# Two expert layers at the end of a metaformer kernel: four pairs of images in the second weight pass, expert outputs copied to token rows by TensorE, and a redrawn order

## The chip, the cores and the metric

The kernel runs on one core of a Trainium2 chip. The metric is the device time of one execution in microseconds (us), the median of several runs.

## What is computed

The input is x with shape (32, 56, 56, 128), fp32: 32 images of 3136 tokens with 128 channels. Two layers follow each other, each with a mixing step and a feed-forward step, all with residuals.

```python
x = x + L0_conv(_ln_c(x))            # batch norm, binarised 3x3 convolution
t = t + L0_ffn(_ln_t(t))             # 8 experts, each token uses its top 2
x = x + L1_conv(_ln_c(x))            # triangle-like product over each image
t = t + L1_ffn(_ln_t(t))             # 64 experts, each expert chooses 8 tokens
```

The change touches the last step. For each image, a softmax over the tokens gives each of the 64 experts its 8 best tokens with weights topv. An expert gets one vector per image, the weighted sum of these 8 tokens, runs it through two layers, and the result is added back to the same 8 tokens:

```python
pooled = jnp.einsum('bked,bke->bed', gathered, topv)
h = jax.nn.gelu(jnp.einsum('ebd,edh->ebh', h, weight1), approximate=False)
out = jnp.einsum('ebh,eho->ebo', h, weight2)
weighted = jnp.einsum('beo,bke->bkeo', out, topv)
outputs = outputs.at[batch, flat_idx].add(weighted)
```

So an expert (128x512 and 512x128 weights, 256 KB each in fp32) sees 32 vectors only, one per image. Two images can choose no common token, but two experts of one image can choose the same token, so additions to one image have to be ordered or summed first.

## The kernel before, in words

Images are handled in 16 pairs; a pair has 7 units of 896 tokens. A first sweep takes statistics of all images for the batch norm (up to about 330 us). Then the pairs flow through a pipeline of stages, several pairs at once: `fetch`, `sign`, `conv`, `conv_back` (convolution), `moe_turn`, `moe_gates`, `moe_experts`, `moe_add` (the 8 experts: a gate row is broadcast from DRAM into a tile gb at line 821, multiplied with the transposed tokens xT on VectorE at line 827, and multiplied with all experts' weights on TensorE at line 832, tile acc), `tri_*` (the product over an image), `gate_stats`, `gate_turn`, `gate_logits` (outputs to DRAM, logits for the 64 experts), `top8` (MAX8 and FIND_INDEX8 on VectorE, lines 1189 and 1193, then 8 gathers of token rows on POOL, line 1222) and `pool_rows` (the pooled vector per expert; its transpose on TensorE is line 1251 for the late pairs).

The 64 experts run in 16 groups of four, in two passes over all weights. The first pass (`late_experts(False, g)`) serves pairs 0 to 12 and begins when pair 12 is pooled; the second (`late_experts(True, g)`) serves the last NL = 3 pairs. Each group is: load weights (lines 1412, 1414), first layer `ph` (1479), a copy on ScalarE, a transpose `trh` (1503), bias (1511) and gelu (1519), second layer `po` (1525), output bias on VectorE (1533), and a store of 128x128 outputs to DRAM (1541).

What follows differs. In the first pass the outputs of a group are loaded back from DRAM, each image's row 8 times, into two tiles eo (line 1551, 8 loads a group on the SP queue; tag xT, the buffers that hold the transposed tokens), multiplied by topv (1558, one VectorE instruction of 112 or 96 rows x 512), and added to token rows in DRAM by 8 indirect DMAs with add (1575, on POOL). The images of the first pass form two lots (0 to 13 and 14 to 25); the scatters of one lot have to follow each other, those of two lots need not. When a scatter belongs to another lot than the one before it, POOL first runs a tiny memset (line 1316).

In the second pass nothing is scattered with add. `last_sums` makes per pair a matrix m of topv where two experts chose the same token (lines 1647, 1655) and gathers that pair's token rows, 8 gathers of 128 rows (1666). `last_load` brings the outputs of 32 experts to SBUF (1689); `last_out_rows` multiplies m by them on TensorE (1708), adds the rows (1720) and writes them with indirect DMAs (1731). It does so in two halves of 32 experts; the second half sums over all 64. Writes of one pair follow each other.

The order is drawn up by the kernel itself. A planner (`Order.run`) plays the whole program with a cost per operation (the numbers given to `op`, and `land` for a DMA's landing), chooses the next operation per engine by a rank, and emits the instructions in the order that results. The ranks come from `TICK`, a table of due times per stage and unit; PERIOD = 14 ticks separate two pairs. On the chip each engine runs its instructions strictly in that order and waits at the first one that is not ready; so does the SP queue with its DMA issues. Tiles come from tags with fixed numbers of buffers (x 15, u 6, ps 8 PSUM banks, gb 5, xT 4).

Of the kernel before, what the change touches and what calls it, by code (L numbers as in the profile page):

```python
# [12 lines left out]
F32 = mybir.dt.float32  # L13
# [14 lines left out]
C = 128  # L28
N7 = 7
# [9 lines left out]
    "fetch": (1.58, 3.45, 5.52, -1.97, 9.89, 8.41, 11.94),  # L39
    "sign": (-0.24, 0.69, 0.62, 6.29, 6.36, 10.44, 7.52),  # L40
    "conv": (1.26, 2.47, 6.82, 8.46, 10.49, 11.27, 13.74),
    "conv_back": (3.04, 3.74, 6.89, 9.11, 10.54, 11.48, 14.87),
    "moe_turn": (4.55, 4.08, 9.93, 10.17, 12.05, 12.07, 15.21),
    "moe_gates": (7.93, 6.46, 10.3, 10.32, 15.22, 13.8, 15.72),
    "moe_experts": (10.11, 8.23, 10.44, 10.38, 15.35, 13.82, 17.26),
    "moe_add0": (14.4, 13.58, 10.89, 13, 17.91, 16.49, 17.47),
    "moe_add1": (12.35, 12.05, 11.31, 12.55, 16.09, 14.74, 18.98),
    "tri_turn": (16.03, 16.94, 19.18, 18.34, 19.2, 18.97, 19.62),
    "moe_stats": (4.06, 9.6, 11.95, 15.11),
    "moe_route": (6.11, 10.25, 12.5, 15.67),  # L50
    "tri_stats": (14.43, 14.07, 18.68, 19.34),
    "tri_b": (20.52, 21.37),
    "tri_a": (22.17, 21.41),
    "tri_z": (22.19,),
    "tri_out": (23.45, 23.11, 25.14, 25.06, 25.81, 28.13, 29.03),
    "gate_stats": (23.81, 25.31, 26.89, 30.24),
    "gate_turn": (25.22, 25.8, 26.84, 28.27, 29.66, 32.16, 31.08),
    "gate_logits": (26.8, 27.15, 28.55, 30.19, 30.4, 34.44, 34.71, 34.72),
    "clear": (32.94,),
    "top8": (36.55,),  # L60
    "pool_rows": (39.18,),
    "late_first": (27.19, 27.47, 30.26, 33.5, 37.45, 38.24, 40.16, 41.35, 43.38, 44.86, 45.85,
        48.06, 49.55, 51.3, 58.28, 60.22),
    "late_alone": (47.43, 50.82, 50.84, 53.47, 61.88, 67.39, 57.81, 65.6, 63.21, 71.67, 75.8,
        82.21, 97.17, 84.67, 68.82, 79.34),
    "last_sums": (70.63, 74.49, 77.96),
    "last_load": (68.66, 101.21),
    "last_rows": (91.82, 76.74, 99.71, 103.42, 119.45, 116.33),
# [4 lines left out]
NX, NY = 15, 6  # L73
# [212 lines left out]
def kernel(ctx: ExitStack, tc: tile.TileContext, a: dict, out: bass.AP):  # L286
# [12 lines left out]
    HB = B // 2  # L299
# [23 lines left out]
    make_identity(nc, ident)  # L323

# [42 lines left out]
    NL = 3  # L367
    LAST = range(NP - NL, NP)
    HB = 2 * ((NP - NL + 1) // 2)
    LOTS = ((0, HB), (HB, B - 2 * NL)) + tuple((2 * p, 2 * p + 2) for p in LAST)  # L370
# [3 lines left out]
    EH = E1 // 2  # L374
# [4 lines left out]
    o_d = [dram.tile([NE, B, C], F32, name=f"o_{g}") for g in range(E1 // NE)]  # L379
# [25 lines left out]
    with ExitStack() as c2:  # L405
# [21 lines left out]
        for t in lines:  # L427
# [3 lines left out]
            "x": NX, "u": NY, "ps": 8, "gb": 5, "xT": 4, "yl": 3,  # L431
            "st": 3, "q": 3, "lg": 1, "k1": 1, "k2": 1, "mk": 2, "d": 2,
            "gg": 2, "gT": 2, "rm": 4, "zq": 1, "lgT": 1,
            "m8": 2, "i8": 2, "sq": 2, "pg": 4, "near": 2, "pacc": 1, "ptc": NL + 1,
# [155 lines left out]
        def fetch(p, u):  # L590
            g = p * NU + u
            x_ = live[p]["x", u] = new("x", [128, N7, C], f"x_{NUT + g}")

            @op("SP", 360, w=parts(x_), land=1200)
            def _():
                nc.sync.dma_start(x_.ap, x_units[g])

        def sign(p, u):
# [3 lines left out]
            @op("SP", 360, r=[("y1_d", g)], w=[y], land=1200)  # L602
            def _():
                nc.sync.dma_start(y.ap, y1_d[g])
# [205 lines left out]
        def moe_experts(p, u, n):  # L810
# [8 lines left out]
            @op("SP", 360, r=[("gd", p, u)], w=[gb], land=1300)  # L819
# [136 lines left out]
        def tri_z(p):  # L956
# [71 lines left out]
            @op("SP", 360, r=[(zT, 0), (zT, 4)], w=[("z_d", p)], land=300)  # L1028
# [12 lines left out]
            for rg in range(4):  # L1041
                @op("SP", 720, r=[("z_d", p), zv], w=[(zv, rg)], land=300)
# [86 lines left out]
        def gate_turn(p, u):  # L1129
# [6 lines left out]
            @op(*issue, r=parts(x_), w=[("out", p, u)], land=1200)  # L1136
# [7 lines left out]
            @op(*issue, r=parts(y), w=[("y3", p, u)], land=1200)  # L1144
# [1009 lines left out]
```

## Time and profile before

| | |
|---|---|
| three timed runs | 3786.0, 3786.38, 3797.89 us (median 3786.38) |
| profiled execution | 3805.24 us, its span 3803.4 us |
| busy of the span | PE 3427.8 us (90%), DVE 3191.5 (84%), ACT 2350.5 (62%), POOL 443.8 (12%) |
| mean granted TensorE clock | 0.96 |
| largest group | acc at L832: 12544 instructions, 1473.6 us |
| scatters of the first pass, L1575 | 128, mean 1548 ns, idle before them 317.1 us |
| loads of eo at L1551 | 128, median 781 ns of the SP queue each |
| DMA | 842 MB, mean 221 GB/s |

PE is TensorE's matmul stream, PEld its weight loads, DVE VectorE, ACT ScalarE, POOL GpSimd, SP the queue that issues most DMAs. In a row of groups or of the timeline, `out<-in` are the program's names, an xN at the end the number of merged instructions, and the bracket the idle time of the engine before it with what ended it. A fp32 matmul is two instructions.

### The profile page before, as it was taken

What the parts mean: (1) busy time and instruction counts of PE and PEld (TensorE: products, weight loads), DVE (VectorE), ACT (ScalarE), POOL (GpSimd) and SP (SyncE); (2) the same over time, 40 slices, a digit from 0 to 9 for tenths busy, and PEclk for the clock granted to TensorE, in tenths of its full rate; (3) what the DMA queues carried; (4) which work ended last, traced back from release to release, by engine and by line L of the source; (5) the groups of instructions that cost most, each with busy time, mean ns of one, the idle gap of its engine ahead of it and who ended that gap; (6) DMA issues with size and microseconds to landing.
All of it is one profiled execution on the core that took longest, in us unless ns stands there. A gap on an engine that the chain in (4) does not pass through costs nothing.

```text
span 3803.4 us, 79485 instructions
## 1 busy us (share of the span) xinstructions
PE 3427.8 (90%) x28051; PEld 2791.8 (73%) x28051; DVE 3191.5 (84%) x10626; ACT 2350.5 (62%) x5438; POOL 443.8 (12%) x506
## 2 busy tenths in 40 slices
PE   7998999999999999999999999999999997876644
PEld 7886878787877777777777777777777775664422
DVE  7997979898989898989898989898989886765551
ACT  6997357575757666666666666666666664453420
POOL 0000000101010101010101010101010104234454
PEclk9999999999999999999999999999999998898667
DMA  7996747474747474747474747474747477687685
GB/s 292 358 356 226 256 155 268 151 272 148 276 150 268 146 268 153 269 154 269 154 269 156 265 155 268 157 267 158 265 160 262 163 251 210 201 248 227 184 238 163
DMA packets 358127, 842.03 MB, mean 221 GB/s; under 512 B 89169, under 2 KB 133154, under 8 KB 357730
## 3 DMA queue, kind: packets, MB, share of 16 engines
q1 hardware_dynamic: 298658, 719.02, 54.8%
q10 hardware_dynamic: 38080, 99.57, 6.6%
q0 software_dynamic: 20992, 18.37, 2.9%
q8 instruction: 223, 3.65, 0.4%
q14 instruction: 174, 1.43, 0.1%
HBM read 661.53 MB, written 175.23 MB: 220 GB/s over the span
## 4 chain that ended last, share of the span: by engine, by line
PE 44%; DVE 27%; DMA 14%; ACT 8%; issue 3%; SPq 2%; POOL 1%; another core or an unknown queue 0%; ACTq 0%; POOLq 0%; DVEq 0%
PE acc L832 21%; DMA gb<-gate 7%; DVE gb L827 5%; DVE stln L488 5%; PE gram L1799 4%; PE ps_cv L633 4%; PE tr L477 3%; PE ps_g L1067 2%; ACT yt L562 2%; DVE frame L611 2%; DVE x L575 2%; DMA w_True<-in_L_ffn_weight 2%; PE ps_z L976 2%; DVE x L1111 1%; DVE sg L1102 1%
## 5 line engine op out<-in xcount | busy, mean ns | idle before, releaser
L832 PE MATMUL acc<-expert_w,gb 128*128 128x128 f32 x12544 | 1473.6, 278 | 73.0 <-DVE gb L827 49.2
L832 PEld LDWEIGHTS acc<-expert_w,gb 128*128 128x128 f32 x12544 | 1437.7, 193 | 121.7 <-DVE gb L827 51.4
L827 DVE TENSOR_TENSOR gb<-gb,xT 128x1024 f32<-128x1024 f32 x784 | 949.3, 1220 | 95.3 <-DMA gb<-gate 91.3
L488 DVE BATCH_NORM_STATS2 stln<-x 128x6 f32<-128x128 f32 x2352 | 600.1, 287 | 1.9
L562 ACT ACTIVATE yt<-x,rmln 128x128 f32<-128x128 f32 x784 | 327.2, 495 | 203.6 <-DVE rmln L550 190.0
L562 ACT ACTIVATE yl<-x,rmln 128x128 f32<-128x128 f32 x756 | 324.2, 494 | 175.7 <-DVE rmln L547 125.3
L633 PE MATMUL ps_cv<-frame,w_sign 128*128 128x448 bf16 x2016 | 420.0, 357 | 8.3 <-DVE frame L611 8.3
L562 ACT ACTIVATE ym<-x,rmln 128x128 f32<-128x128 f32 x784 | 324.6, 486 | 66.9 <-DVE rmln L550 57.3
L633 PEld LDWEIGHTS <-w_sign 128*128 128x128 bf16 x2016 | 196.5, 98 | 174.4 <-DVE frame L611 8.5
L1222 POOL DMA_INDIRECT rows<-y,near x128 | 133.2, 1041 | 995.5 <-DVE k L738 795.7
L1575 POOL DMA_INDIRECT out<-eo_False,picked x128 | 198.1, 1548 | 317.1 <-DMA out<-eo_False,picked 137.0
L1118 POOL MEMSET a_bd<- 128x2048 f32 x15 | 27.1, 1807 | 1655.4 <-PE ps_zo L1089 1655.4
L562 ACT ACTIVATE y<-x,rm 128x128 f32<-128x128 f32 x448 | 210.5, 716 | 14.5 <-DVE rm L547 14.5
L1067 PE MATMUL ps_g<-wg,yT 128*128 128x128 f32 x1568 | 211.2, 283 | 0.0
L1067 PEld LDWEIGHTS ps_g<-wg,yT 128*128 128x128 f32 x1568 | 192.0, 195 | 20.5 <-issue 12.0
L583 ACT COPY xT<-trm 128x512 f32<-128x512 f32 x224 | 110.1, 529 | 151.6 <-PE trm L477 132.7
L641 ACT ACTIVATE cv<-ps_cv,cv_shift,cv_scale 128x448 f32<-128x448 f32 x224 | 159.2, 726 | 70.7 <-PE ps_cv L633 36.1
L844 DVE TENSOR_TENSOR x<-acc,x 128x512 f32<-128x512 f32 (+1 forms) x224 | 139.7, 623 | 73.7 <-PE acc L832 62.8
L1799 PE MATMUL gram<-y 128*128 128x128 f32 x1568 | 198.4, 279 | 0.0
L1799 PEld LDWEIGHTS gram<-y 128*128 128x128 f32 x1568 | 194.4, 200 | 0.5 <-issue 0.5
L488 DVE BATCH_NORM_STATS2 st<-x 128x6 f32<-128x128 f32 x784 | 179.6, 282 | 4.6 <-DMA x<-in_x 4.6
L583 ACT COPY ylT<-trl 128x512 f32<-128x512 f32 x224 | 113.7, 533 | 111.4 <-PE trl L477 102.0
(263 smaller groups left out, 5439.5 us busy)
## 6 DMA issues: line engine op xcount, KB each, us to landing
gb<-gate SPq DMA_DIRECT2D x784, 512.0 KB
x<-in_x SPq DMA_DIRECT2D x224, 448.0 KB
y<-yT SPq DMA_DIRECT2D x112, 448.0 KB
ys<-y SPq DMA_DIRECT2D x112, 448.0 KB
out<-x ACTq DMA_DIRECT2D x105, 448.0 KB
y<-yl ACTq DMA_DIRECT2D x105, 448.0 KB
w_False<-in_L_ffn_weight SPq DMA_DIRECT2D x128, 256.0 KB
w_True<-in_L_ffn_weight SPq DMA_DIRECT2D x102, 256.0 KB
```

What stands on the lines that cost most here:

```text
L488: nc.vector.bn_stats(st.ap[:, c0 + k, :], src.ap[:, k, :])
L562: nc.scalar.activation(dst.ap[:, k, :], src.ap[:, k, :], AF.Identity, bias=m, scale=r)
L583: nc.scalar.copy(t.ap[:, n0 : n0 + k, :].rearrange("c n p -> c (n p)"), ps.ap[:, : k * 128],)
L633: nc.tensor.matmul(acc, lhsT=w_sign[:, tap, :], rhs=frames[f][:, 8 * band + kh : 8 * band + kh + 8, kw : kw + W], start=(tap == 0), stop=( ...
L641: nc.scalar.activation(cv.ap[:, :, 64 * h : 64 * h + 64], ps.ap[:, :448].rearrange("c (q n) -> c n q", n=N7), AF.Identity, bias=cv_shift, ...
L827: nc.vector.tensor_tensor(gb.ap, gb.ap, over(xT.ap[:, n, :], E0), ALU.mult)
L832: nc.tensor.matmul(acc.ap[:, n % 4 * C : (n % 4 + 1) * C], lhsT=gb.ap[:, e, :], rhs=expert_w[:, e * C : (e + 1) * C], start=(e == 0), stop ...
L844: nc.vector.tensor_tensor(dst, acc.ap[:, : k * C], dst, ALU.add)
L1067: nc.tensor.matmul(psg.ap[:, n * C : (n + 1) * C], lhsT=yT[:, n0 + n, 16 * u : 16 * u + 16, :].rearrange("c r v -> c (r v)"), rhs=wg, star ...
L1222: nc.gpsimd.indirect_dma_start(out=rows.ap[:, j, :], out_offset=None, in_=y3_d[p], in_offset=bass.IndirectOffsetOnAxis(ap=near.ap[:, k + j ...
L1575: ins = nc.gpsimd.indirect_dma_start(out=tokens_out, out_offset=bass.IndirectOffsetOnAxis(ap=picked[lot][:rows, e : e + 1], axis=0), in_=e ...
L1799: nc.tensor.matmul(gram.ap[:, :C], lhsT=y.ap[:, n, :], rhs=y.ap[:, n, :], start=(g % G16 == 0 and n == 0), stop=(g % G16 == G16 - 1 and n ...
```

## The change

The number of pairs in the second pass goes from 3 to 4, so the first pass serves pairs 0 to 11 and its two lots are 12 images (96 rows) each. The first pass keeps its outputs on the chip: a constant `spread` of 128 x 2 x 96, built at the start from the identity by 8 VectorE copies, is multiplied on TensorE with the outputs of each expert (32 rows), which gives each image's row 8 times in PSUM; VectorE multiplies by topv on the way to eo, now per expert and lot, in 4 buffers of a tag of its own; xT has 3 buffers. The store to DRAM and the loads back go away in the first pass. In the second pass the final rows are made for 48 experts first and then for 16, and the fourth pair's rows live in eo buffers. Landing times given to the planner change at many DMAs, and all of TICK is redrawn, for the early stages as well.

```diff
-    "late_first": (27.19, 27.47, 30.26, 33.5, 37.45, 38.24, 40.16, 41.35, 43.38, 44.86, 45.85,
-        48.06, 49.55, 51.3, 58.28, 60.22),
+    "late_first": (27.83, 31.72, 32.41, 37.47, 41.1, 43.48, 47.62, 49.5, 49.91, 52.26, 56.62,
+        60.45, 61.11, 64.22, 76.21, 94.35),
...
-NX, NY = 15, 6
+NX, NY, NEO = 15, 6, 4
...
+    NL = 4
+    spread = const.tile([128, 2, HB * K1], F32, name="spread")
+    for q in range(0, 128, B):
+        for k, (i0, i1) in enumerate(LOTS[:2]):
+            nc.vector.tensor_copy(
+                spread[q : q + B, k, : (i1 - i0) * K1].rearrange("b (i k) -> b i k", k=K1),
+                along(ident[q : q + B, q + i0 : q + i1], K1),
+            )
...
-    NL = 3
-    EH = E1 // 2
+    PARTS = ((0, 1, 2), (3,))
...
-            "x": NX, "u": NY, "ps": 8, "gb": 5, "xT": 4, "yl": 3,
+            "x": NX, "u": NY, "ps": 8, "gb": 5, "xT": 3, "yl": 3, "eo": NEO,
...
-            @op("SP", 360, w=parts(x_), land=1200)
+            @op("SP", 360, w=parts(x_), land=1262)
...
-            @op("SP", 360, r=[pt], w=[("pooled", p)], land=1500)
+            @op("SP", 360, r=[pt], w=[("pooled", p)], land=5600)
...
-                @op("SP", 720, r=[("o_d", g)], w=[eo], land=300)
-                def _(eo=eo, i0=i0, i1=i1, rows=rows):
-                    for j in range(NE):
-                        nc.sync.dma_start(
-                            eo.ap[:rows, j, :],
-                            o_d[g][j, i0:i1, :].unsqueeze(1).to_broadcast([i1 - i0, K1, C]),
+            for j in () if alone else range(NE):
+                ps_e = bank(f"ps_eo_{name}_{j}")
+
+                @op("PE", 2 * 222, r=[(side2, "o")], w=[ps_e])
+                def _(q=B * j, ps_e=ps_e):
+                    for k, (i0, i1) in enumerate(LOTS[:2]):
+                        rows = (i1 - i0) * K1
+                        nc.tensor.matmul(
+                            ps_e.ap[:rows, k * C : (k + 1) * C],
+                            lhsT=spread[q : q + B, k, :rows], rhs=side2.ap[q : q + B, 5, :],
+                            start=True, stop=True,
                         )
-                @op("DVE", 600, r=[("picked", p) for p in range(i0 // 2, i1 // 2)], w=[eo])
-                def _(eo=eo, lot=lot, rows=rows):
-                    nc.vector.tensor_tensor(
-                        eo.ap[:rows, :NE, :], eo.ap[:rows, :NE, :],
-                        along(gains[lot][:rows, es], C), ALU.mult,
-                    )
+                eo = new("eo", [128, 2, C], f"eo_{name}_{j}")
+                for lot in range(2):
+                    @op(
+                        "DVE", 230, r=[ps_e] + [("picked", p) for p in range(i0 // 2, i1 // 2)],
+                        w=[(eo, lot)],
+                    )
+                    def _(eo=eo, lot=lot, rows=rows, e=e, ps_e=ps_e, k=lot):
+                        nc.vector.tensor_scalar(
+                            eo.ap[:rows, lot, :], ps_e.ap[:rows, k * C : (k + 1) * C],
+                            gains[lot][:rows, e : e + 1], None, ALU.mult,
+                        )
...
-        def last_load(half):
+        def last_load(part):
-            groups = range(half * E1 // NE // 2, (half + 1) * E1 // NE // 2)
+            e0, e1 = 16 * PARTS[part][0], 16 * PARTS[part][-1] + 16
...
-            @op("PE", 4 * 222, r=[m] + [(at, "o", h) for h in range(half + 1)], w=ps)
+            @op("PE", 2 * n * 222, r=[m] + [(at, "o", h) for h in range(part + 1)], w=ps)
```

## The prediction

> **What bounds the kernel now.** I read the page first, then busy time by stretches cut at the starts of MAX8 (line 1189, the step that closes a pair of images), then the waits, then the timeline. The page says that TensorE is busy for 90% of the span, in two very different parts:
>
> ```profile
> PE   7998999999999999999999999999999997876644
> PEclk9999999999999999999999999999999998898667
> ```
>
> Each digit is 95 us. TensorE is full until about 3130 us and then thins out, and its granted clock with it. The stretches put numbers on that. Columns: length, then busy us of PE, PEld, DVE, ACT and POOL with instruction counts, then clock, DMA share, GB/s.
>
> ```profile
> 2789.00:2979.50 190.50, 183.19 (x1514) 150.71 (x1512) 175.04 (x550) 125.07 (x282) 11.74 (x10) 1.00 0.60 212
> 2979.50:3182.40 202.90, 184.18 (x1494) 146.79 (x1493) 169.05 (x519) 125.24 (x271) 26.44 (x22) 0.96 0.65 215
> 3182.40:3455.50 273.10, 219.07 (x1738) 169.91 (x1737) 177.96 (x555) 137.37 (x284) 99.60 (x112) 0.88 0.74 214
> 3455.50:3624.70 169.20, 106.58 (x833) 75.74 (x833) 86.11 (x280) 76.93 (x139) 82.86 (x99) 0.72 0.74 212
> 3624.70:3803.40 178.70, 73.43 (x753) 40.39 (x753) 62.84 (x176) 25.14 (x38) 84.61 (x123) 0.70 0.66 192
> ```
>
> The first row is a steady pair: 190.5 us, 183.2 of them TensorE at full clock. It is TensorE's own work, and only 7 us per pair could be won there. The loss is in the rows below. From pair 12's MAX8 (2979.5) to the last expert matmul of pair 15 (the timeline has it end at 3486.4) 507 us pass. To say how much work that is, I counted matmuls in the program order of TensorE, with one duration per kind from merged timeline rows (48 acc instructions in 5.52 us, 14 ps_g in 1.72, 7 transposes in 0.93, 9 conv in 1.89). The stretch holds 414 us so counted, a steady pair holds 198 and takes 190.5, so at steady pace it would take 398 us. **The excess is 109 us**, and it starts with the first scatter of the late experts (3127). The waits of 2979.5 to 3624.7 (total, times, longest) say what it hangs on:
>
> ```profile
> SPq L1551 <- DMA out<-eo_False,picked: 51.3, 7, 9.7
> DVE eo_False L1558 <- DMA eo_False<-o: 46.0, 15, 13.1
> DVE gb L827 <- DMA gb<-gate: 33.1, 26, 3.4
> PE acc L832 <- DVE gb L827: 27.6, 12, 9.0
> ```
>
> One instance from the timeline, a row per queue:
>
> ```profile
> 3154.71 3.18 SPq L1551 DMA_DIRECT2D eo_False<-o  x4
> 3159.75 0.69 DVE L1558 TENSOR_TENSOR eo_False<-eo_False,gains 96x512 f32<-96x512 f32 x1 [7.49 <-DMA eo_False<-o]
> 3163.49 2.93 PE L832 MATMUL acc<-expert_w,gb 128*128 128x128 f32 x12 [8.97 <-DVE gb L827]
> ```
>
> SP issues nothing between 3144.9 and 3154.7, because its next load needs an eo buffer that scatters still hold; then VectorE stands 7.49 us at the multiply of that eo; then TensorE stands 8.97 us for a product that VectorE has behind it. The round trip of expert outputs through DRAM (lines 1541, 1551, 1558) stops the main pipeline through two in-order queues.
>
> After pair 15's MAX8 another thing rules: weights for all 64 experts. TensorE's first matmul of the second pass is at 3652, the last weight load leaves SP at 3764.9, and then come the row writes:
>
> ```profile
> 3782.09 0.97 POOL L1731 DMA_INDIRECT out<-rows_last,at_last  x1 [6.85 <-DVE rows_last L1720]
> 3783.05 0.09 POOL L1316 MEMSET between<- 1x1 f32 x1
> 3783.36 0.97 POOL L1731 DMA_INDIRECT out<-rows_last,at_last  x1 [0.23 <-DVE rows_last L1720]
> ```
>
> A write costs 1.27 us of POOL, since each is of another lot than the one before and brings a memset. The twelfth starts at 3796.1 and the span ends 7.3 us later.
>
> **The change, part by part**, against the profiled execution (span 3803.4, time 3805.2; the three timed runs have a median of 3786.4, 0.5% less, and I carry a difference in us over to it unscaled).
>
> *Order of the steady pairs.* All ticks are redrawn, but work per pair is the same, the order of pairs 0 to 11 shows the same stages at about the same distances, and one buffer fewer for xT is what the new order was drawn for. TensorE sets the pace; 7 us of idle per pair is the most to win. I take 0, with 15 either way over 12 pairs. The set-up of "spread" is 8 copies of 32x96; the nearest row is line 1466's 0.19 us for 128x104, so 1.5 us, between the identity (ready at 2.1 us) and VectorE's first statistics at 4.17, which wait for a DMA. Nothing; without that cover 1.5.
>
> *Copies on TensorE.* 128 fp32 matmuls, each two instructions, 32 rows by 96 columns by 128. By the new order those of 11 groups, 88 matmuls or 176 instructions, fall before pair 15's last expert matmul; the rest lie in the drain, where TensorE has room. The nearest row is the one for last rows with 32-row operands:
>
> ```profile
> 3750.12 1.90 PE L1708 MATMUL ps_last<-at_last,last_m 32*128 32x128 f32 x24
> ```
>
> That is 0.079 us per instruction; full 128x128 ones (14 in 1.72) take 0.123. The Trainium skill, "TensorE: Matmul & The Clock Gate", section "Why this matters for your kernels", speaks against the change here: a matmul over 32 rows takes as long as one over 128, and only tiles in distinct row groups run side by side. By the first half the sum is 176 x 0.123 = 22 us. The four experts of a group lie in four row groups, next to each other in the order, so the second half (4 row tiles measured there at 3.07 times) would give 7 us. I take the row: 176 x 0.079 = 14 us, and 4 us because the order counts 4 us more of other work before that point (group 10 lies wholly ahead of it): **+18**, 11 to 26.
>
> *A new wait on TensorE.* The copies need the bias add (line 1533, 0.29 us) that itself needs the last matmul of the group. In the trace po ends at 3317.85 and the add at 3320.0, 2.1 us. The new order leaves a median of 0.9 us of TensorE work between the two (0 to 4.6); summing the shortfalls over the 11 groups gives 8 us. Behind the waiting copy stands all of TensorE, mostly expert matmuls. **+8**, 4 to 20.
>
> *VectorE.* Away: 32 multiplies of 0.69, 22 us. New: 128 multiplies of 96x128 out of PSUM; nearest row line 1533 with 0.29, so 37 us (planned at 0.23: 29). Plus the sums of a fourth pair, 8 x 0.55 + 7 x 0.69 = 9 us, in the last stage where VectorE is busy for 63 of 179. In the dense part +13 us over three pairs lie beside TensorE (VectorE 175 of 190): 0, at most 13.
>
> *The round trip goes.* Away are 144 SP issues (128 of 0.78 us, 100 us of SP) and every row above but the third, which was its consequence in part. TensorE's own idle time put on late products is 27.6 us; both queues' stalls as if never overlapping are 97. Of the excess of 109, part belongs to the weight loads and scatters themselves, which stay. With less idle time the clock also holds, which the 0.88 row charges. I take **-60**, bounds -28 and -97. What is late next: gb loads that wait for gates (SP, 47.2 us).
>
> *The first pass starts a pair earlier.* Only pairs 0 to 11 are needed, so by the new order 4 groups stand before the place where the old order has its first, and the 16 groups spread over 70% more TensorE work (575 us counted against 338). Their own cost moves, and does not change; its value is inside the -60. Scatters remain 128, now 96 rows in both lots.
>
> *Drain of pair 15* (3486 to 3624.7, 138 us). Of the chain of waits in 3455.5 to 3624.7, SP line 1551 has 8.2%, eo loads 6.1% and scatters 5.5%, together 33 us of 169. In the new order 126 of 128 scatters stand ahead of pair 15's pooled transpose (119 before). **-20**, 0 to -33.
>
> *The last stage.* By the order 73 of 128 half-expert loads follow the pooled transpose instead of 77: (3764.9 - 3651.7)/77 = 1.47 us each, -6. Eight more reads and one more broadcast are 0.8 MB at about 200 GB/s, +4, which fewer left-over scatters give back. But the writes get worse: the matmuls for the first 48 experts now stand behind the last group's first matmul (3767.3 today), and their 24 writes and the last 8 are 32 x 1.27 = 41 us, begun some 3 us later, against first writes of the last dozen at 3782.1 and 15 us of them. From that matmul to the last issue: 44 now, 30 before. +14. Together **+9**, 0 to 20.
>
> Sum: 0 + 18 + 8 - 60 - 20 + 9 = **-45 us**: span 3758, and 3741 for the median.
>
> **The rivals.**
> - *Forecast, 3741 (range 3710 to 3772), chance 0.48.*
> - *The excess goes nearly whole*: -97 and -33, since the first pass has three pairs to hide in. 18 + 5 - 97 - 33 + 5 gives -102: 3684, with a share of it up to 3710. For it: no stretch before 3120 shows such losses. Against: weight loads and scatters share the DMA queues as before. Chance 0.14.
> - *The next wait takes over*: only TensorE's 27.6 us and a little of the drain are won because gb loads still come late behind gate writes: 18 + 8 - 28 - 10 + 9 is -3: 3783, within 0.3%. Chance 0.12.
> - *Slower: scatters hold eo's four buffers, and VectorE waits at the head of its queue.* The first scatters of a lot stand 11.6, 6.4, 6.0 and 9.8 us apart in the trace. A group has four per lot, so 25 to 35 us; the new order puts groups 6, 7, 8 only 17 to 20 us of TensorE work apart and 11, 12, 13 only 4. It decides once a lot's scatters take over 5 us where groups are close. Seven groups late by 10 to 12 us are +75; -45 + 75 is +30: 3816. Against: scatters of alternating lots later ran 1.8 us apart (3.6 per lot). With a redrawn order that keeps less in hand per pair (1 us over 12 pairs is +12) it is the same side. Chance 0.26.
>
> Faster means over 0.3%, that is under 3775, about what a measurement of this kernel can tell from no change: 0.48 + 0.14, less a little for the forecast's edge, 0.61; same 0.13; slower 0.26. The range takes the forecast, most of both neighbours and half of the slow case: 3695 to 3815.
>
> **What would show it.** Right: MAX8 to MAX8 still 190 to 191 us in the steady part; no VectorE wait on eo loads, no SP wait on scatters; idle of the copies near 1 us a group; expert matmuls ending near 3486 + 18 + 8 - 60 = 3452 instead of 3486; POOL issuing row writes without pause at 1.27 us to the end. Wrong: VectorE waits at the new multiplies for scatters (slow case), TensorE still waiting for gb as long as now (third case), or steady pairs off by over 1 us.

## The result and the profile after

The changed kernel takes 3821.4 us (median of 5 runs, 3819.7 to 3823.5); the kernel before, beside it, 3797.9 (3786.0 to 3807.5). The ratio is 1.0064, 95% interval 1.0039 to 1.0089: slower, where 3741 us was forecast. The profiled span is 3818.4 us against 3803.4, so +15.0 us where the sum said -45. (The profiled execution of the kernel before was a long one, 3805.2 us; between the medians the difference is 23.5 us.)

The page's rows for TensorE and its clock in forty slices, now 95.5 us each:

```profile
PE   7998899999999999999999999999999999998633
PEclk9999999999999999999999999999999999999766
```

The thin end is shorter: TensorE stays full for 36 slices instead of 33. The stretches cut at MAX8 show what that cost (columns as before: length, busy us of PE, PEld, DVE, ACT, POOL, clock, DMA share, GB/s):

```profile
2656.40:2852.80 196.40, 186.09 (x1517) 153.23 (x1514) 175.59 (x551) 126.15 (x281) 13.14 (x10) 0.98 0.60 206
2852.80:3048.90 196.10, 183.74 (x1536) 150.20 (x1533) 173.59 (x543) 128.36 (x282) 28.88 (x25) 0.99 0.60 204
3048.90:3256.10 207.20, 194.83 (x1694) 153.18 (x1692) 175.51 (x587) 138.84 (x290) 69.59 (x74) 0.98 0.75 237
3256.10:3498.60 242.50, 224.41 (x1957) 181.13 (x1957) 198.90 (x622) 145.39 (x305) 97.52 (x106) 0.96 0.80 245
3498.60:3622.10 123.50, 87.76 (x730) 61.60 (x729) 75.64 (x273) 67.91 (x124) 50.30 (x66) 0.79 0.70 216
3622.10:3818.40 196.30, 75.17 (x829) 40.77 (x829) 74.40 (x222) 25.72 (x40) 90.11 (x131) 0.66 0.56 164
```

The first row is a steady pair: 196.4 us, and its clock is 0.98, no longer 1.00. From MAX8 of pair 1 to that of pair 11 a pair took 191.2 us before (876.6 to 2789.0) and 196.9 now (884.1 to 2852.8). Pair 12's MAX8 comes at 3048.9 instead of 2979.5, **69.4 us late**. Behind it, pairs 13 to 15 take 573.2 us instead of 645.2 (-72.0), and the last stage 196.3 instead of 178.7 (+17.6). So 69.4 - 72.0 + 17.6 is the whole +15.0. The late part gained, 54 us in all; the 12 pairs that the change was not about lost more than that.

The waits of pairs 13 to 15 (3048.9 to 3622.1; total, times, longest), first those of VectorE, then those of TensorE:

```profile
DVE eo_False L1575 <- DMA out<-eo_False,picked: 7.3, 2, 4.0
```

```profile
PE acc L838 <- DVE gb L833: 9.2, 10, 3.4
```

VectorE's wait for eo loads (46.0 us before) is gone with the loads, scatters hold the new eo buffers for 7.3 us only, and TensorE waits 9.2 us for gated tokens instead of 27.6. From pair 12's MAX8 to the end TensorE is busy for 582 us, 583 before, and idle for 187 instead of 241: the 54 us are idle time.

The ten steady pairs from MAX8 of pair 1 to that of pair 11, before and after:

```profile
876.60:2789.00 1912.40, 1835.80 (x15122) 1507.37 (x15120) 1748.19 (x5490) 1250.61 (x2801) 117.24 (x100) 1.00 0.60 211
884.10:2852.80 1968.70, 1854.17 (x15125) 1527.90 (x15122) 1756.59 (x5492) 1262.21 (x2801) 131.49 (x100) 0.99 0.59 205
```

TensorE's idle time (length less busy) went from 76.6 to 114.5 us, and its busy time for the same matmuls from 1835.8 to 1854.2. Of the 5.7 us that a pair lost, 3.8 are idle and 1.8 busy time. TensorE's largest wait there before, and the wait that matters below:

```profile
PE acc L832 <- DVE gb L827: 15.9, 24, 1.3
...
PE trc L477 <- ACT cv L641: 0.3, 1, 0.3
```

and after:

```profile
PE trc L483 <- ACT cv L647: 38.7, 25, 3.2
PE acc L838 <- DVE gb L833: 25.3, 39, 1.5
```

Most of the first row is one place per pair: ten waits of 3.05 to 3.25 us make 31 of the 38.7. In the timeline this place is a chain over four engines:

```profile
2288.00 1.61 POOL L1045 MEMSET zv<- 128x1792 f32 x1
2288.77 0.87 DVE L556 TENSOR_SCALAR rmln<-rmln 128x7 f32<-128x7 f32 x1
2289.68 0.49 ACT L568 ACTIVATE yt<-x,rmln 128x128 f32<-128x128 f32 x1 [3.04 <-DVE rmln L556]
2290.38 0.72 ACT L647 ACTIVATE cv<-ps_cv,cv_shift,cv_scale 128x448 f32<-128x448 f32 x1
...
2291.16 1.76 PE L483 MATMUL trc<-ident,cv 128*128 128x128 f32 x7 [3.09 <-ACT cv L647]
```

A tiny add on VectorE runs beside a memset on POOL and takes 0.87 us (0.17 is the median of this line). ScalarE has an activation at the head of its queue that needs the sum, and the copy of cv stands behind that activation. TensorE waits 3.09 us for the copy. Stretches of 4 us around it show the clock (third column from the right):

```profile
2288.00:2292.00 4.00, 0.91 (x5) 0.84 (x5) 3.20 (x15) 2.32 (x7) 1.61 (x2) 0.78 0.06 16
2292.00:2296.00 4.00, 4.00 (x24) 2.57 (x26) 3.52 (x16) 2.48 (x6) 0.00 (x0) 0.50 0.05 14
2296.00:2300.00 4.00, 4.00 (x36) 1.59 (x32) 1.52 (x9) 3.17 (x7) 0.00 (x0) 0.86 0.63 212
```

At the end of the gap and behind it the granted clock is 0.50. Summed over the clock records of the ten pairs, 23.9 us of full clock were withheld, against 1.7 before, in spells of 3.4 or 6.8 us. Nine of the twelve spells begin within 2 us of the end of this gap. The other three follow a gap of 1.0 us at another place (line 1095, which waits for VectorE's sg).

### The profile page after: what moved, and what is told of

It is laid out like the page before. It is cut to its first block, busy times and chain, and to the rows that moved or that the text cites. A ratio compares the mean times of both kernels' runs of the same rounds, so it can differ in the third digit from the quotient of the medians.

```text
span 3818.4 us, 80001 instructions
## 1 busy us (share of the span) xinstructions
PE 3436.8 (90%) x28322; PEld 2803.9 (73%) x28322; DVE 3228.9 (85%) x10767; ACT 2371.1 (62%) x5441; POOL 490.1 (13%) x544
## 4 chain that ended last, share of the span: by engine, by line
PE 45%; DVE 30%; ACT 10%; DMA 8%; issue 5%; ACTq 1%; POOL 1%; SPq 0%; another core or an unknown queue 0%; DVEq 0%; POOLq 0%
PE acc L838 22%; DVE gb L833 7%; DVE stln L494 5%; PE gram L1843 4%; PE ps_cv L639 4%; PE tr L483 3%; DMA ys<-y 3%; DVE sg L1108 2%; DMA gb<-gate 2%; ACT ym L568 2%; DVE x L1117 2%; PE ps_z L982 2%; DVE x L581 2%; ACT yl L568 2%; ACT cv L647 1%
## 5 line engine op out<-in xcount | busy, mean ns | idle before, releaser
L838 PE MATMUL acc<-expert_w,gb 128*128 128x128 f32 x12544 | 1494.1, 278 | 65.6 <-DVE gb L833 46.2
L494 DVE BATCH_NORM_STATS2 stln<-x 128x6 f32<-128x128 f32 x2352 | 567.5, 289 | 2.2
L568 ACT ACTIVATE ym<-x,rmln 128x128 f32<-128x128 f32 x784 | 335.3, 492 | 163.0 <-DVE rmln L556 137.0
L1228 POOL DMA_INDIRECT rows<-y,near x128 | 157.1, 1228 | 818.4 <-DVE x L850 683.2
L1124 POOL MEMSET a_bd<- 128x2048 f32 x15 | 27.6, 1840 | 1751.2 <-PE ps_zo L1095 1393.0
L568 ACT ACTIVATE y<-x,rm 128x128 f32<-128x128 f32 x448 | 210.3, 715 | 12.0 <-DVE rm L553 11.5
L1073 PE MATMUL ps_g<-wg,yT 128*128 128x128 f32 x1568 | 204.2, 280 | 0.5 <-ACT ylT L589 0.5
L850 DVE TENSOR_TENSOR x<-acc,x 128x512 f32<-128x512 f32 x224 | 139.0, 620 | 69.3 <-PE acc L838 65.9
L494 DVE BATCH_NORM_STATS2 st<-x 128x6 f32<-128x128 f32 x784 | 187.4, 284 | 4.2 <-DMA x<-in_x 4.1
L581 DVE TENSOR_TENSOR x<-trc,x 128x512 f32<-128x512 f32 x224 | 133.2, 619 | 67.5 <-PE trc L483 66.5
L1083 ACT ACTIVATE sg<-ps_g 128x512 f32<-128x512 f32 x224 | 115.2, 535 | 120.9 <-PE ps_g L1073 106.6
```

The costliest lines, as they stand in the source:

```text
L494: nc.vector.bn_stats(st.ap[:, c0 + k, :], src.ap[:, k, :])
L568: nc.scalar.activation(dst.ap[:, k, :], src.ap[:, k, :], AF.Identity, bias=m, scale=r)
L581: nc.vector.tensor_tensor(xf, ps.ap[:, : k * 128], xf, ALU.add)
L838: nc.tensor.matmul(acc.ap[:, n % 4 * C : (n % 4 + 1) * C], lhsT=gb.ap[:, e, :], rhs=expert_w[:, e * C : (e + 1) * C], start=(e == 0), stop ...
L850: nc.vector.tensor_tensor(dst, acc.ap[:, : k * C], dst, ALU.add)
L1073: nc.tensor.matmul(psg.ap[:, n * C : (n + 1) * C], lhsT=yT[:, n0 + n, 16 * u : 16 * u + 16, :].rearrange("c r v -> c (r v)"), rhs=wg, star ...
```

## The experiments

My first theory: the loss is this one place (the wait and the half-clock spell behind it). The rival: the redrawn order as a whole, at many places. Seventeen runs of thirteen kernels, on four chips, which the tables call A to D; the kernel before took a median of 3784.2 on A, 3798.0 and 3799.4 on B, 3796.1 on C and 3801.2 on D, so ratios are compared and not times.

**1 and 2. The ticks of the early stages exchanged** (chip A). In the changed kernel the rows `fetch` to `pool_rows` of TICK are those of before (1); in the kernel before they are those of after (2).

> The changed kernel, but the rows of TICK from fetch to pool_rows are those of the kernel before; the rows from late_first on, four late pairs, copies on TensorE, three xT buffers and the new landing times stay. Theory 1 (the redrawn order of the early stages costs 5.8 us a pair): MAX8 to MAX8 back to 190 to 192 us, no wait of trc on cv, and the late part keeps most of its 54 us: total 3735 to 3770. Rival A (three xT buffers or the landing times cost it): a pair stays at 195 to 198 and the total at 3805 to 3830. Rival B (old ticks and late part do not fit each other): a pair at 191, but the late part loses over 30 of its 54 us: 3775 to 3800.

> The kernel before, with the rows of TICK from fetch to pool_rows of the changed kernel; three late pairs, the round trip through DRAM, four xT buffers and the old landing times stay. Theory 1: a pair takes 195 to 198 us, and the total is 3850 to 3880. Rival A (xT buffers or landing times are needed for the loss): a pair at 190 to 193, total 3790 to 3815. A middle value means that the place of the loss depends on the planner's replay and not on the ticks alone.

3935.9 us, 1.0414 [1.0398, 1.0429], and 3923.0, 1.0378 [1.0360, 1.0396]; 204.2 and 199.9 us a pair. Every theory missed. The ticks of one plan put beside the other plan's landing times and buffers give orders worse than both. The stretch of pairs 13 to 15 still took 572.2 us in run 1: its gain does not need the new order of the early stages.

**3. One activation moved** (A). ScalarE's first yt activation of one unit stands behind the second copy of cv.

```diff
+            k = self.mark[f"yt_{p}_6", 0]
+            i = out.index(k)
+            acts = [n for n in range(i + 1, i + 60) if ops[out[n]][0] == "ACT"][:4]
+            hit = [n for n in acts if out[n] in cvs]
+            if hit:
+                out.insert(hit[0], out.pop(i))
```

> The changed kernel with one instruction per pair moved on ScalarE: the first normalisation of unit 6 for the triangle step (yt) is emitted behind the second convolution result (cv) instead of ahead of it; all else in its order. Theory 2 (the loss is this one place: ScalarE stands at yt for VectorE's statistics, cv waits behind it, TensorE stands 3.1 us at trc, and its clock is halved for some 7 us after): the 3 us gaps of trc go, the clock of the steady part is 1.00, a pair takes 190 to 192.5, total 3750 to 3775. Rival (the loss is spread over many small waits of the new order): a pair at 194 to 196, total 3795 to 3815.

3781.4 us, 0.9995 [0.9983, 1.0007]. The wait shrank, and the ten steady pairs became a little shorter:

```profile
PE trc L494 <- ACT cv L660: 17.2, 23, 1.0
```

```profile
883.70:2842.80 1959.10, 1855.62 (x15124) 1521.38 (x15120) 1755.74 (x5492) 1260.63 (x2801) 131.29 (x100) 0.99 0.60 206
```

The wait is 21.5 us less and the withheld clock fell from 23.9 to 10.2 us. If these counted in full, the ten pairs would be 21 us (the wait alone) to 35 us (both) shorter; they are 9.6 us shorter. Idle time fell by 11.0 us only, because other waits grew, and busy time did not fall at all (1855.6). So the withheld clock is not what lengthened the busy time here.

**4. The add as tensor_tensor** with a tile of ones, where the trace shows tensor_scalar held by the memset (A).

```diff
-fns.append(lambda: ts(nmr(), nmr(), plus, None, ALU.add))
+fns.append(lambda: tt(nmr(), nmr(), ones[:, :n], ALU.add))
```

> The changed kernel; the add of 1 to the means in the second and third norms (line 556) is a tensor_tensor with a constant tile of ones instead of a tensor_scalar. In the trace this tensor_scalar ends with POOL's memset of zv, 0.87 us instead of 0.17, once a pair, ahead of yt. If the collision with the memset decides, the gap of trc shrinks from 3.1 to about 2.4 us; if that already keeps the clock up, a pair takes 191 to 193 and the total is 3755 to 3785; if not, only 0.7 us a pair: 195.5 to 196, total 3808 to 3818. If the operation does not matter, no change: 3818 to 3824.

3785.7 us, 1.0010 [0.9999, 1.0020]. The longest wait for cv is 2.5 us instead of 3.2, as expected, and the add no longer feels the memset:

```profile
2284.70 1.61 POOL L1048 MEMSET zv<- 128x1792 f32 x1
...
2285.36 0.15 DVE L558 TENSOR_TENSOR rmln<-rmln,ones 128x7 f32<-128x7 f32 x1
```

Both times, 36 to 40 us below the changed kernel's first ones, lie near what the one-place theory asked for. But MAX8 to MAX8 was still 195.9 and 196.2 us, 1.0 and 0.7 less than the changed kernel's. That is 8 to 12 us over 12 pairs; the other 25 or more had to come from somewhere else. The kernel before is itself 14 us faster on A than in the first comparison. And the last stage took 170 us in both runs, and 196 in the changed kernel, with nothing changed there. So the changed kernel was run again.

**5 to 8** (chip B): the changed kernel unaltered (5); the changed kernel with before's ticks of the early stages, before's landing times of the steady pairs and of the first sweep, and four xT buffers, in which the eo tiles lie too (6); edits 3 and 4 together (7); kernel 6 with three pairs in the second pass (8).

```diff
-            "x": NX, "u": NY, "ps": 8, "gb": 5, "xT": 3, "yl": 3, "eo": NEO,
+            "x": NX, "u": NY, "ps": 8, "gb": 5, "xT": 4, "yl": 3,
...
-                eo = new("eo", [128, 2, C], f"eo_{name}_{j}")
+                eo = new("xT", [128, N7, C], f"eo_{name}_{j}")
```

> The changed kernel once more, unaltered, beside the kernel before on the same chip as the next three. In its one profile the weight loads of the late experts stand still for 13 us at 3709 us and the last stage takes 196 us; the two kernels with one small edit each, whose late order is nearly the same, took 170. If the stand-still belongs to the kernel (its five times lay within 4 us), the ratio is 1.006 again and the last stage is 190 to 200 us: about 3808 beside 3784. If it was an event of that one chip or set of runs, the last stage is 170 us and the time 3785 to 3800: then what the two small edits gained in the 12 steady pairs is 1 us a pair or less, not the 36 to 40 us that their times seem to show.

> The changed kernel with everything of the order planner that touches the steady pairs set back to before: ticks of the stages up to the pooled rows, landing times of the activations and gates, four buffers of xT. The eo tiles lie in the xT buffers to make room. Its TensorE order is then that of before, instruction for instruction, over the first 6734 of 8578 rows; the copies, four pairs, parts of 48 and 16 stay. Theory order: the whole loss of 69 us lies in the order of the steady pairs: MAX8 to MAX8 is 190.5 to 191.5 us again and the time 3725 to 3755 with a late part like after's. Theory shared resources (the steady pairs lose to something that the change does elsewhere, not to their order): 196 us a pair stay and the time is 3790 or more. Theory late part tied to the new order: the pairs are at 191, but the late part, planned with ticks drawn for another order, is 40 us or more longer than after's: 3770 to 3800.

> Both small edits at once: one normalisation instruction of ScalarE moved behind the second copy of cv, and the add of 1 as tensor_tensor. If the wait of the transposes on cv and the half-clock spell behind it were the main loss of the steady pairs, both together give 192 to 193 us a pair and 3735 to 3760. If each alone gained only 1 us a pair (as their MAX8 spacing of 195.9 and 196.2 shows), both give 195 to 195.5 us a pair and 3770 to 3785: the loss is then spread over many places of the order.

> As the run with the old steady order, but with three pairs in the second weight pass and thirteen in the first (the number NL, and its rows of the plan). The round trip stays away, copies stay. Prediction's sum: taking the fourth pair back costs the 20 us of pair 15's drain less about 4 us of the last stage: 10 to 20 us slower than the run with four. If the gain of the late part is all in the fourth pair: 40 us or more slower. If it is all in the round trip: within 8 us.

(5) 1.0058 [1.0044, 1.0072]: the result repeats, 196.8 us a pair, last stage 200. (7) 1.0039 [1.0026, 1.0051] with 196.0 us a pair: **the one-place theory falls**, as far as the edits reach. On this chip the wait at that place is down from 3.1 to 2.0 us a pair, all waits on cv to 27.6 us, the withheld clock to 13.7, and the pair gains 0.8 us. TensorE's busy time does not follow the clock here either: 1853.2 us in ten pairs, and 1852.7 in run 5, where 22.2 us were withheld. Run 3 went further, to waits of 1.0 us, and gained 1.0. No run takes the wait away altogether. (6) settles the steady pairs:

```profile
2408.80:2600.20 191.40, 183.56 (x1514) 150.78 (x1512) 174.99 (x550) 124.77 (x281) 11.84 (x10) 1.00 0.61 211
```

191.6 us a pair on average, as before the change, with copies, four pairs and 48 and 16 all in place. TensorE's sequence of matmuls in these pairs agrees with that of before in the traces of 6, 8, 9, 10 and 17, and a pair takes 190.5 to 191.6 us in all five. The loss of the steady pairs is their order. Yet 6 takes 3823.8 us, 1.0060 [1.0046, 1.0074]: its late part is 831 us long, 59 more than in 5. A possible reason is in the trace: with eo in the xT buffers, VectorE stands 41.0 us for scatters in pairs 13 to 15, where it stands 7.3 in the changed kernel. (8) 3792.3, 0.9980 [0.9974, 0.9987]: with three pairs it is 31 us faster than with four, against my -20 for the fourth.

**9 to 12** (chip D): the plan of before with the round trip replaced by copies and nothing else of the change (9); that with four pairs (10); the kernel before with only the landing times of the steady pairs and of the first sweep changed (11); the kernel before with three xT buffers (12).

```diff
-            "x": NX, "u": NY, "ps": 8, "gb": 5, "xT": 4, "yl": 3,
+            "x": NX, "u": NY, "ps": 8, "gb": 5, "xT": 3, "yl": 3,
```

(That is 12; 11 sets `land` to 1262, 1392, 1150 and 800.)

> One part alone: the plan of before (all its ticks and landing times, three pairs in the second pass, last writes in two halves of 32 experts), but the late experts' outputs are copied by TensorE and scaled straight out of PSUM, with no trip through memory; the eo tiles lie in the xT buffers. The TensorE order is that of before over its first 7190 of 8639 rows. The prediction's terms for this part are -60 for the round trip (-28 to -97), +18 for the copies, +8 for their wait: 34 us faster than before, 0.991, all of it after the MAX8 of pair 12. Rival: the next wait takes the place of the round trip: within 8 us of before, with the VectorE and SP idle time moved to other rows. Rival from the run with the old order and three pairs, whose late part was 15 us shorter than before's: 0.996 to 0.998.

> As the run with the round trip alone, and pair 12 in the second weight pass too (four pairs; ticks of the added rows put between their neighbours). The prediction's terms: -20 for the drain of pair 15 in the first pass, +4 of the last stage: 16 us faster than the run with the round trip alone. Theory that the four pairs need a plan of their own (the run with the old steady order and four pairs had a late part 22 us longer than the one with three): 15 to 35 us slower than it.

> The kernel before with one input of its planner as after the change: the landing times of the loads and stores of the steady pairs (1262 for 1200 ns, 1392 for 1300, 1150 and 800 for 300 twice), with the ticks of before. Nothing else is changed, the program differs by its order alone. If the loss of the steady pairs is that an order drawn from other inputs is worse by chance of the draw: 194 to 206 us a pair and 3840 to 3960. If the order follows the ticks and the landing times hardly count: 190.5 to 192 us a pair and within 10 us of before.

> The kernel before with three buffers of xT for four, its ticks and landing times kept. TensorE's order is then the same as before in most of the steady part. If the missing buffer is what costs 5.7 us a pair: 194 to 197 us a pair and 3840 to 3870. If three are enough for the steady pairs: 191 to 192 us a pair, and up to 20 us more in the late part, where the buffers hold expert outputs in this kernel: 3785 to 3815 on the chip where before takes 3798.

(9) 3779.9 us, **0.9947 [0.9927, 0.9966]**: faster than both kernels, 21 us where the terms gave 34. Pairs 13 to 15 take 634.7 us, only 10 less than before. VectorE's largest wait there says why:

```profile
DVE eo_False L1575 <- DMA out<-eo_False,picked: 72.7, 21, 8.6
```

With eo in the xT buffers, scatters hold them and VectorE stands: the mechanism of the slow rival, in place of the 46.0 us for loads. (10) 1.0170 [1.0154, 1.0186]: 87 us slower than 9; the ticks between which pair 12's rows were put were not drawn for four pairs, so this prices a bad plan and not the fourth pair. Its steady pairs take 190.7. (11) 3988.6 us, 1.0494 [1.0477, 1.0512], 204.3 us a pair: landing times alone redraw everything, to the worst order of all. (12) 3910.2, 1.0268 [1.0246, 1.0290]. An early and a later pair of 12:

```profile
921.00:1120.00 199.00, 191.46 (x1528) 157.32 (x1526) 174.30 (x546) 127.98 (x286) 11.76 (x10) 0.97 0.59 203
1524.30:1715.20 190.90, 183.72 (x1516) 151.09 (x1514) 174.54 (x550) 124.83 (x281) 11.55 (x10) 1.00 0.61 212
```

Three buffers are enough: once the order has settled into that of before, the pair takes 190.9. Where TensorE's order differs, in the first four periods, it takes 199 to 206.

**13 to 17: the last stage.** In the changed kernel's last stage TensorE and SP nearly stand still for 33 us:

```profile
3696.40 0.71 SPq L1420 DMA_DIRECT2D w_True<-in_L_ffn_weight  x1
3697.84 0.37 PE L1531 MATMUL po_True<-frame,hG_True 128*32 128x128 f32 x1 [2.42 <-issue]
...
3699.95 0.37 PE L1531 MATMUL po_True<-frame,hG_True 128*32 128x128 f32 x1 [1.74 <-issue]
```

The stretch in the changed kernel, and about the same place in run 3 on A:

```profile
3690.00:3722.00 32.00, 4.83 (x13) 1.65 (x13) 2.13 (x4) 0.00 (x0) 20.66 (x25) 0.50 0.46 140
```

```profile
3680.00:3720.00 40.00, 25.89 (x227) 11.15 (x220) 23.23 (x55) 5.97 (x10) 13.33 (x15) 0.71 0.95 296
```

In the changed kernel TensorE runs a matmul every 2 to 3 us and waits for nothing that the profile shows ("issue"): 13 in 32 us, where run 3 has 227 in 40. To find out whether this comes with the kernel: last writes in two halves again (13) and the unaltered kernel (14), both on B; then the unaltered kernel (15), kernel 3 (16) and kernel 9 (17) side by side on C.

```diff
-    PARTS = ((0, 1, 2), (3,))
+    PARTS = ((0, 1), (2, 3))
```

> The changed kernel with its last writes in two halves of 32 experts again; TensorE's order is the same over its first 8544 of 8578 rows. The prediction gave the last stage +9 us in all for four pairs and 48 and 16 experts. If the parts of 48 and 16 bring their share (fewer row writes behind the last sum): halves are 4 to 10 us slower than the changed kernel on the same chip. If the write of rows on GpSimd, 32 of them after the last sum at 1.27 us each, is what ends the kernel either way: within 3 us.

> The changed kernel once more, as the base of the run with halves. If the stand-still of TensorE and SP for 33 us in the second weight pass comes with the kernel: ratio 1.005 to 1.007 and a last stage of 190 to 200 us, as in both profiles so far. If it comes with the chip: ratio 0.997 to 1.001 and a last stage near 170 us on a chip without it.

> The changed kernel once more, beside the kernel with one moved instruction of ScalarE on the same chip. If the stand-still comes with the program and where its instructions lie: it is here (last stage 190 to 200 us, ratio 1.004 to 1.007) and not in the other (170 us). If it comes with the chip: it is in both or in neither, and both last stages agree within 5 us.

> The kernel with one normalisation instruction of ScalarE moved behind the second copy of cv, on the same chip as the unaltered changed kernel. Its steady pairs are 195.9 us again (1 us less a pair than the changed kernel's 196.9, 10 to 12 us in all). If the stand-still comes with the program: 35 to 40 us faster than the changed kernel on this chip. If it comes with the chip: 8 to 14 us faster.

> The version with the old plan and the round trip's removal alone, on the same chip as the changed kernel: 0.993 to 0.997 of before again, 30 to 45 us faster than the changed kernel if that shows its stand-still here, 10 to 20 if not.

(13) 1.0063 [1.0045, 1.0082] and (14) 1.0054 [1.0034, 1.0073]: last stages of 199.7 and 198.3 us, no difference that can be told. (14) fell on B again and decided nothing about chips. (15) 1.0061 [1.0037, 1.0085], last stage 200.7. (16) 1.0049 [1.0031, 1.0066], last stage 202.1, where the same kernel had 170.1 on chip A. Its timeline here:

```profile
3698.31 0.37 PE L1546 MATMUL po_True<-yT,hG_True 128*32 128x128 f32 x1 [2.43 <-issue]
```

So the same program stands still on C and not on A. What decides lies outside the program: the chip, or something else that differed between the two sets of runs. Runs 3 and 4 owed most of their apparent gain to that, since the last stage of this kernel and its near kin is 26 to 32 us shorter on A; against the changed kernel on its own chip, edit 3 is worth 6.6 us, with five and four runs whose spreads overlap. The changed kernel itself was not run on A. With 12 pairs of 1.0 or 0.7 us added back, runs 3 and 4 give an estimate of 3793 to 3794 us there, 0.2 to 0.3% above the kernel before. By this estimate over half of the 0.6% hangs on where the kernel runs. (17) 0.9964 [0.9946, 0.9981], 39 us faster than the changed kernel beside it.

| kernel (run, chip) | us a pair, MAX8 1 to 11 | MAX8 12 to 15 | last stage | ratio to before |
|---|---|---|---|---|
| before | 191.2 | 645.2 | 178.7 | 1 |
| after, first comparison | 196.9 | 573.2 | 196.3 | 1.0064 |
| after (5 B, 14 B, 15 C) | 196.8, 196.8, 196.8 | 572, 568, 571 | 200, 198, 201 | 1.0058, 1.0054, 1.0061 |
| one activation moved (3 A, 16 C) | 195.9, 196.2 | 564, 571 | 170, 202 | 0.9995, 1.0049 |
| tensor_tensor (4 A), both (7 B) | 196.2, 196.0 | 570, 570 | 170, 196 | 1.0010, 1.0039 |
| old steady order (6 B), three pairs (8 B) | 191.6, 190.5 | 637, 591 | 195, 218 | 1.0060, 0.9980 |
| round trip alone (9 D, 17 C) | 191.1, 190.7 | 635, 642 | 164, 169 | 0.9947, 0.9964 |
| round trip alone with four pairs (10 D), after in halves (13 B) | 190.7, 196.6 | 669, 572 | 187, 200 | 1.0170, 1.0063 |
| ticks exchanged (1 A, 2 A) | 204.2, 199.9 | 572, 678 | 172, 162 | 1.0414, 1.0378 |
| before with landing times (11 D), with three xT (12 D) | 204.3, 194.2 | 654, 661 | 190, 194 | 1.0494, 1.0268 |

The kernel before has one profile, of the first comparison, and none on A to D. Differences from its row compare chips as well as kernels; the ratios do not.

## Why the prediction was wrong

- **The step that failed: "Order of the steady pairs ... I take 0, with 15 either way over 12 pairs."** It measured +69.4 us. I saw that work per pair and the distances of the stages were the same and that TensorE sets the pace, and took that for the same time. But a pair's 7.7 us of idle time was an achievement of the old order: the new one has 11.5, and it keeps TensorE busy 1.8 us longer with the same matmuls. Runs 6, 8, 9, 10 and 17 show that the order is the cause: with the old steady order the changed code needs 190.5 to 191.6. None of the four other redraws, each from inputs changed in part, came out as good: runs 1, 2 and 11 cost 9 to 13 us a pair on average, and run 12 cost 8 to 15 where its order differed. My own test, "steady pairs off by over 1 us", was the right one; 12 pairs make 1 us count twelvefold, and the slow rival named this, but as a side remark with +12.
- What in the new order costs it is settled in part. The wait for cv is the largest row (38.7 us in ten pairs), yet shortening it, from 3.1 us to between 1.0 and 2.5, gave 0.6 to 1.0 us a pair of 5.7. That the rest is spread over many small waits is argued, not shown. Why the same matmuls keep TensorE busy longer was not found.
- The clock. The Trainium skill, "TensorE: Matmul & The Clock Gate", section "Why this matters for your kernels", advises against idle gaps over about 3 us between bursts of matmuls. At one place the trace agrees: a gap of 3.09 us, then 0.50. But the runs also have half-clock spells behind shorter gaps: of 1.0 us in three of the changed kernel's twelve, of 1.2 to 1.3 in all six of run 6, of 2.0 at most in run 7. So no gap here is known to be short enough. I read 1.00 in the old rows and did not ask what margin it had; but run 3 more than halved the withheld clock without shortening the busy time, so the clock is not the main cost.
- **The stretch of pairs 13 to 15**: +18 +8 -60 -20 was -54, it measured -72.0. The sum came out near by luck: its costs were too high and its parts are not proven. The copies take 11.5 us of TensorE time in 224 instructions, 0.051 us each where the prediction took 0.079, and their wait is 2.4 us, so +18 and +8 were high. The round trip alone (9, 17) gave only -10 and -3 there, where VectorE waits for scatters. In the changed kernel it hardly does (7.3 us), with eo buffers of its own and groups planned further apart. Kernel 8 reached -54 in this stretch with the new late ticks, three pairs and 35.8 us of that wait, and gave 39 us of it back in the last stage. Run 1, with own eo buffers and another early order, kept 572; run 6, with eo in the xT buffers, lost it (637). That would fit the buffers, but run 3 has 26.8 us of the wait for scatters and a stretch of 564. How much of the -72 is the fourth pair, how much the own buffers and how much the late ticks stays open: no run changes one of them alone in the changed kernel.
- **The last stage**, +9, measured +17.6. The mechanism (32 writes at 1.28 us each to the end) was right but for one pause of 4.2 us, as these rows show, the first write, the one behind the pause and the last:

```profile
3766.80 0.99 POOL L1775 DMA_INDIRECT out<-rows_last,at_last  x1 [49.91 <-DVE rows_last L1758]
...
3802.65 0.97 POOL L1775 DMA_INDIRECT out<-rows_last,at_last  x1 [4.16 <-DVE rows_last L1758]
...
3810.31 0.97 POOL L1775 DMA_INDIRECT out<-rows,at_last  x1 [0.22 <-issue]
```

  From the first write to the end of the last 44.5 us pass; 44 were forecast, counted from a matmul a little earlier. The size of the stage depends on where it runs: 170 us for near kin on A, 196 to 202 on B and C, where the stand-still falls into it. The sum had no term for that.
- The rivals. The "next wait takes over" and "excess goes nearly whole" cases did not happen. The slow rival gave 3816 by scatters that hold eo. That it lies 5 us from the result is luck: that wait is 7.3 us in the changed kernel. Its side remark carried the sign.

## What to carry to other kernels

Where a planner draws the order, every input (a landing time, one buffer less) is a change to the whole program: multiply 1 us per repetition by the repetitions before pricing the part that the change is about, and keep the tuned order of the steady part when only the tail is to be changed. Here that version (9, 17) wins 0.4 to 0.5%, where the full change loses 0.5 to 0.6% on B and C. Before a single place is called the cause, look at the repeated period itself: total time can fall for another reason, such as another chip. And a wait that shrinks is not yet time won: in run 3 half of it came back as other waits.

## What the runs showed of the hardware

- A VectorE tensor_scalar of 128x7 fp32 took 0.87 us beside a POOL memset, and 0.15 us as tensor_tensor beside the same memset (run 4). The longest of 128 such instructions took 0.98 and 0.19. The Trainium skill, "VectorE: DVE Perf Modes", section "Mode 2×_2P — use both read ports for one tensor", lets only operations with a single tensor input use both ports; "Advanced Engine Details and Errata", section "Mode Summary", says that the second port is shared with GpSimd and that the two block each other. The two durations agree with that.
- One program, two chips: TensorE and SP slowed for about 33 us, at the same place in every profile of the changed kernel and its near kin on B and C (runs 5, 7, 13 to 16) and in the first comparison, never on A (3, 4). In the profiles of the first comparison and of run 5 a 16 KB transfer of the instruction queue starts 0.5 us before the first slow matmul, and most of SP's issues take 0.70 us instead of 0.33 in that time. Such a transfer alone is not the cause: run 3 has one at 3679.4 and goes on at its pace. What holds the two engines was not found.
- The half-clock spells of the steady pairs last 3.41 us or a multiple of it (up to 13.65 in run 11). They do not come in every pair, though the order of each pair is the same: 12 spells in ten pairs of the changed kernel, 10 in its next run. Kernel 3 lost 10.2 us of clock on A and 18.8 on C, where its wait for cv was also longer: 27.5 us in ten pairs instead of 17.2.
